# Other blocks transposed on TensorE, and another list of rank shifts for the planner, in a post-norm transformer block

## The chip, the core and the metric

The kernel runs on one core of a Trainium2 chip, as a single launch. The metric is the device time in microseconds of one execution. A core has five engines with queues of their own: TensorE (PE in the profile; PEld is its weight load), VectorE (DVE), ScalarE (ACT), GpSimd (POOL) and SyncE (SP), which here only issues transfers. All data is float32.

## The reference, cut to what matters

Two batches of 512 tokens of width 512 go through one layer:

```python
x = layernorm(x + attention(x))      # 32 query heads, 8 key/value heads, head size 128
x = layernorm(x + ffn(x))            # width 1376, silu(gate) * up, int32 weights with scales
# attention: q, k = rmsnorm(x Wq^T), rmsnorm(x Wk^T); v = x Wv^T
#            softmax(q k^T / sqrt(128) + slope_h * (j - i), masked to j <= i) v, then Wo
```

Every product over 512 or more is a matmul on TensorE. Transposes are needed twice in attention: the normed heads (so that the head size lies on partitions) and the probabilities (so that the keys lie on partitions).

## The kernel before

**Tiles.** A unit is one block of 128 tokens of one batch and one key/value head (group) `g` with its 4 query heads: `units` has 8 x 2 x 4 = 64 entries, and two neighbouring units make one of the 32 `pairs`. For each pair, `project` computes q, k and v of 256 tokens as seven products of half-size blocks (Strassen's scheme, `seven`, banks `pa`, `pb`, `pc`), with sums of blocks (`sums_x` of x, `sums_q` of the weights) made on DVE and POOL; pair 0 is projected by plain products (`project_plain`, bank `pp`, L856). `heads` squares, averages and norms the heads (`sq`, `ms`, `inv`), and turns them into `qT` and `kT`. `scores` computes a unit's scores (`sc`, L1252), the running maximum on DVE (L1261), the exponentials on ACT (L1277) and the division by the sum. `attend` turns the probabilities (`prT`) and multiplies by v (`pa`, L1397); the second unit of the last pair of a group also does the halves `px` and `pz` (L1429). `project_out`/`project_pair` multiply by Wo, `norm1` norms, and `ffn_up`/`ffn_down` follow. Batch 0 can start its feed-forward part while batch 1 is still in attention.

**Two ways of turning.** By default heads and probabilities are turned without TensorE: DVE transposes 32x32 squares (`squares`, L957, tile `st`; L1177 for heads), SP writes them to DRAM (`far`, L966; `far_q`, L1190) and reads them back in the order wanted (`prT`, L1374; `qT`, L1201). For the pairs in `NEAR = {0, 31}` TensorE transposes them instead (`ptq` and `ptk`, L1134 and L1149, 10 for a pair; `pt`, L1348), and DVE or ACT copies them out. Pairs in `NEAR` need their v in another row order (`vn`, loaded by SP).

**What sets the order.** Nothing is issued as it is written. `Work.add` collects about 8000 pieces of work, each with a rank (`prio`), its possible engines and a cost; `Work.order` places them one by one: among the ready ones, the one that can start first, then the one of lowest rank. So the engine for a piece, the order on each queue and the buffer are all a result of the ranks. Before that, `Work.shift` is called for each number in `SHIFTS`: the number seeds a random generator that draws a place in the ranks and moves the ranks of all work near it by random amounts. Loads have ranks too, so their order on the SP and ACT queues moves with them. The first loads are the four pieces of x (`load_x`, ACT queue, 128 rows each of `xT`, of which the first is split in two halves) and of the first group's weights (`load_qkv`, SP queue), rank -9 and up.

**Semaphores of transfers.** Each transfer signals one of eight semaphores in turn, over both queues; a transfer that is to use a semaphore again first waits, in its queue, for the one eight places before it to land.

Of the kernel before, what the change touches and what calls it, by code (L numbers as in the profile page):

```python
# [31 lines left out]
NQ = P // Q  # L32
# [6 lines left out]
LN_EPS = 1e-5  # L39
NEG_INF = -1e30  # L40
MAX_INIT = 3e38
NEAR = {0, 31}
PLAIN = 1
DEEP = HKV - 2
EARLY = 4
# [26 lines left out]
def pool_ts(n):  # L72
# [3 lines left out]
LAG = {"PE": 0.22, "DVE": 0.1, "ACT": 0.12, "POOL": 0.2, "SP": 0.1, "ACTQ": 0.1, "NONE": 0.0}  # L76
TABLE = 1.28
SHIFTS = (
    22000003, 22000016, 22000019, 22000030, 22000031, 22000059, 22000062, 22000085, 22000096,
    22000110, 22000180, 22000208, 22000219, 22000282, 22000333, 22000351, 22000369, 22000431,  # L80
    22000607, 22000642,
)
NORMED = {"DVE": dve(5 * HD) + 0.2, "POOL": pool_tt(5 * HD), "ACT": 5 * act(HD, True)}
WHO = ("DVE", "POOL", "ACT")
# [258 lines left out]
def post_ln_block(  # L343
# [110 lines left out]
    pairs = units[::2]  # L454
    NP = len(pairs)
    NU = len(units)
# [518 lines left out]
    def heads(p, prio):  # L975
# [67 lines left out]
        for r in range(2):  # L1043


            def normed(e, r=r):
                dst = sq[:, r]
                src = c(r)[:, : 5 * HD].rearrange("p (h d) -> p h d", h=G + 1)
                if p in NEAR:
                    dst = dst.rearrange("p h (r m) -> p h m r", m=NQ)  # L1050
                    src = src.rearrange("p h (m r) -> p h m r", m=NQ)
                if e == "ACT":
                    for h in range(G + 1):
                        nc.scalar.activation(  # L1054
                            dst[:, h], src[:, h], AF.Copy, scale=inv[:, r, h : h + 1]
                        )
                    return
                norms = inv[:, r].unsqueeze(2)
                if p in NEAR:
                    norms = norms.unsqueeze(3)  # L1060
                vec[e].tensor_tensor(dst, src, norms.to_broadcast(list(src.shape)), ALU.mult)

            W.add(
                {k: NORMED[k] for k in WHO},
                prio,
                normed,
                [(cb, (r, 0)), (cb, (r, 1)), (inv, r)],
                [(sq, r)],
                port=True,
            )  # L1070
# [2 lines left out]

        v2 = Buf(r_vs, f"vs_{p}")
        v2s[p] = v2
        users = [q for q in range(NP) if pairs[q][:2] == (g, b) and pairs[q][2] >= i]
        if any(q in NEAR for q in users):
            if (g, b) not in vns:
                vns[g, b] = Buf(r_v, f"vn_{g}_{b}")
            vn = vns[g, b]  # L1080
            for m in range(NQ):
                at = H2 * (m // 2) + m % 2
                load(
                    0.13 / NQ,
                    prio + 0.2,
                    lambda q, m=m, at=at, vn=vn: q.dma_start(
                        vn[ts(m, Q), i : i + 2, :], cb[at : at + H2 - 1 : 2, :, 1, 2 * HD :]
                    ),
                    [(vn, (i + r, m)) for r in range(2)],
                    [(cb, (r, 1)) for r in range(2)],  # L1090
                )
        if p in NEAR:
            for m in range(2):
                load(
                    0.02,
                    prio + 0.2,
                    lambda q, m=m: q.dma_start(
                        v2[H2 + m * Q : H2 + (m + 1) * Q, :], cb[m:H2:2, 0, 1, 2 * HD :]
                    ),
                    [(v2, m)],  # L1100
                    [(cb, (0, 1))],
                )
        else:
            copy_op(
                HD,
                prio + 0.2,
                lambda: v2[H2:, :],
                lambda: c(0)[:H2, 5 * HD :],
                [(cb, (0, 1))],
                [(v2, m) for m in range(2)],  # L1110
                ("ACT", "POOL"),
            )
        if any(q not in NEAR for q in users):
            if (g, b) not in vs:
                vs[g, b] = Buf(r_v, f"v_{g}_{b}")
            v = vs[g, b]
            for r in range(2):
                copy_op(
                    HD,
                    prio + 0.2,  # L1120
                    lambda r=r, v=v: v[:, i + r, :],
                    lambda r=r: c(r)[:, 5 * HD :],
                    [(cb, (r, 1))],
                    [(v, (i + r, m)) for m in range(NQ)],
                    ("ACT", "POOL"),
                )
        qT = qTs[p] = Buf(r_qT, f"qT_{p}")
        if p in NEAR:
            for r in range(2):
                pt = Buf(r_po, f"ptq_{p}_{r}")  # L1130

                def transposes(e, r=r, pt=pt):
                    for h in range(G):
                        nc.tensor.transpose(pt[:, ts(h, P)], sq[:, r, h, :], ident.tile)  # L1134

                W.add({"PE": G * TR}, prio + 0.4, transposes, [(sq, r), A(ident)], [A(pt)])
                copy_op(
                    S,
                    prio + 0.4,
                    lambda r=r: qT[:, r, :, : G * Q].rearrange("p a (h c) -> p a h c", h=G),  # L1140
                    lambda pt=pt: pt.tile.rearrange("p (h a c) -> p a h c", h=G, a=NQ),
                    [A(pt)],
                    [(qT, r)],
                )
            ptk = Buf(r_po, f"ptk_{p}")

            def transposes_k(e):
                for r in range(2):
                    nc.tensor.transpose(ptk[:, ts(r, P)], sq[:, r, G, :], ident.tile)  # L1149

            W.add({"PE": 2 * TR}, prio + 0.4, transposes_k, [(sq, 0), (sq, 1), A(ident)], [A(ptk)])

            def evict_k(e):
                dst = kT[:, i * P : (i + 2) * P].rearrange("p (m k r) -> p m k r", m=4, k=2)
                src = ptk[:, : 2 * P].rearrange("p (m r k) -> p m k r", m=4, k=2)
                if e == "ACT":
                    nc.scalar.activation(dst, src, AF.Copy, scale=kw[:, g, :])
                else:
                    nc.vector.tensor_scalar_mul(dst, src, kw[:, g, :])

            W.add(
                {"DVE": 0.48, "ACT": act(2 * P, True)},
                prio + 0.4,
                evict_k,
                [A(ptk), (kw, g)],
                [(kT, (i + r, x)) for r in range(2) for x in range(2)],
            )
            return
# [154 lines left out]
    def attend(u, prio):  # L1323
# [6 lines left out]
        key = f"{g}_{b}_{i}"  # L1330
        pr = pr_of[i]
        p, r = divmod(units.index(u), 2)
        values = lambda q: (vns if q in NEAR else vs)[g, b]
        v = values(p)
        for j in range(i + 1):
            prT = prTs[u, j] = Buf(r_prT, f"prT_{key}_{j}")
            a0 = 2 if j == i and r == 0 else 0
# [2 lines left out]
                reads += [(pr, ("x", a)) for a in range(2)]  # L1340

            n = (NQ - a0) * Q
            if p in NEAR:
                pt = Buf(r_po, f"pt_{key}_{j}")

                def transposes(e, j=j, pt=pt, a0=a0):
                    for a in range(a0, NQ):
                        nc.tensor.transpose(pt[:, ts(a - a0, P)], pr[:, a, ts(j, P)], ident.tile)  # L1348

                W.add({"PE": (NQ - a0) * TR}, prio, transposes, reads + [A(ident)], [A(pt)])  # L1350
                copy_op(
                    NQ * n,
                    prio,
                    lambda prT=prT, n=n: prT[:, : G * n].rearrange("p (h a q) -> p a h q", h=G, q=Q),
                    lambda pt=pt, n=n: pt[:, : G * n].rearrange("p (a h q) -> p a h q", h=G, q=Q),
                    [A(pt)],
                    [(prT, 0), (prT, 1)],
                )
                continue
# [65 lines left out]
        def halves(e):  # L1425
            for m, (q, j) in enumerate(both):
                prT = prTs[(g, b, j), j]
                for k, (bank, val) in enumerate(zip(banks, (values(q)[:, j, :], v2s[q].tile))):
                    nc.tensor.matmul(  # L1429
                        by_head(bank[:, ts(m, S // 2)]),  # L1430
                        lhsT=val[k * H2 : (k + 1) * H2],
                        rhs=by_head(prT[k * H2 : (k + 1) * H2, :])[:, :, :H2],
                        start=True,
                        stop=True,
                        tile_position=(k * H2, 0),
                        skip_group_check=True,
                    )

        reads = []
        for q, j in both:  # L1440
            reads += [(prTs[(g, b, j), j], m) for m in range(2)]
            reads += [(values(q), (j, m)) for m in range(NQ)] + [(v2s[q], m) for m in range(2)]
        W.add({"PE": 1.07}, prio + 0.4, halves, reads, [A(bank) for bank in banks])
        for m, (q, j) in enumerate(both):
            for k, bank in ((1, banks[0]), (0, banks[1])):
# [356 lines left out]
    for p in range(NP):  # L1802
# [3 lines left out]
        if p > 0 and fresh:  # L1806
            load_qkv(g, u - 14.0)
            load_o(g, u - 10.0)
        if p < PLAIN:
            project_plain(p, u - 2.4)  # L1810
        if fresh:
            sums_q(g, u - 3.0)
        if p > 0:
# [417 lines left out]
```

## Time and profile before

| | |
|---|---|
| median of 3 runs | 965.06 us (964.11 to 968.87) |
| profiled execution | 966.59 us, span 964.8 us |
| TensorE busy | 946.9 us, 98% of the span |
| VectorE, ScalarE, GpSimd busy | 75%, 50%, 54% |
| mean granted TensorE clock | 0.996 |
| transfers | 154.83 MB, 160 GB/s |

The page of the profile gives the busy time of each engine, then 40 slices of the span; a waits view lists, for each engine and line, what it sat idle for; a timeline lists instructions in order of time, neighbours of one kind merged, with the idle time before them in brackets. A float32 matmul instruction stands as two records. In a timeline the rows of a queue end in q (SPq, ACTq).

### The profile page before, as it was taken

How to read it: one execution, taken by the hardware profiler on the slowest of the kernel's cores; microseconds unless marked ns; L12 is line 12 of the kernel's file. 1: busy time of each engine (PE TensorE's matmuls, PEld its weight loads, DVE VectorE, ACT ScalarE, POOL GpSimd, SP SyncE). 2: the span in 40 equal slices, each digit the busy share in tenths (PEclk: the TensorE clock that was granted, in tenths of full speed). 3: DMA queues.
4: the chain of work that ended last, by engine and by line, in shares of the span. 5: the costliest groups of instructions: out<-in, count | busy, mean ns of one | idle time of the engine just before them, and what ended most of it. 6: DMA issues, size and time to landing. Idle time of an engine off the chain costs nothing.

```text
span 964.8 us, 14143 instructions
## 1 busy us (share of the span) xinstructions
PE 946.9 (98%) x4274; PEld 684.9 (71%) x4274; DVE 724.6 (75%) x1791; ACT 482.9 (50%) x1343; POOL 516.8 (54%) x587
## 2 busy tenths in 40 slices
PE   9899999999999999999999999999999999999997
PEld 5555666767666676667677767676777888878886
DVE  7777787878887888878877878777776766587554
ACT  3665655545764666555664655545653343434000
POOL 4752765475566658654674877765663522142120
PEclk9999999999999999999999999999999999999999
DMA  8258577555765586884747787567561323310001
GB/s 313 73 190 237 162 233 213 165 156 187 208 208 175 161 249 188 227 236 127 220 141 222 211 239 222 162 188 206 169 199 34 99 67 88 86 48 23 12 33 43
DMA packets 193099, 154.83 MB, mean 160 GB/s; under 512 B 27680, under 2 KB 176160, under 8 KB 191744
## 3 DMA queue, kind: packets, MB, share of 16 engines
q1 hardware_dynamic: 192160, 153.28, 53.3%
q8 instruction: 34, 0.56, 0.3%
q10 hardware_dynamic: 864, 0.66, 0.2%
q14 instruction: 41, 0.34, 0.1%
HBM read 96.28 MB, written 57.15 MB: 159 GB/s over the span
## 4 chain that ended last, share of the span: by engine, by line
PE 91%; DMA 4%; DVE 3%; issue 1%; SPq 0%; ACT 0%; ACTq 0%; POOLq 0%; DVEq 0%; POOL 0%
PE pa_q L736 16%; PE sc L1252 13%; PE pa L1397 11%; PE pa_h L736 8%; PE pb_q L736 8%; PE pa_o L1621 7%; PE pb_h L736 4%; PE pc_q L736 4%; PE pb_o L1621 4%; PE pa_d L736 4%; PE pa_o L736 2%; DMA prT<-far 2%; PE pc_h L736 2%; PE pc_o L1621 2%; PE pb_d L736 2%; PE px L1429 2%
## 5 line engine op out<-in xcount | busy, mean ns | idle before, releaser
L1277 ACT ACTIVATE pr<-pr,nmax 128x48 f32<-128x48 f32 (+15 forms) x256 | 133.2, 521 | 89.0 <-DVE nmax L1261 88.1
L1252 PE MATMUL sc<-kT,qT 128*128 128x176 f32 (+15 forms) x512 | 153.0, 408 | 0.9 <-ACT kT L1215 0.8
L1261 DVE CUSTOM_DVE_ANT_0 pr<-sc,bias 128x48 f32<-128x48 f32 (+15 forms) x256 | 110.0, 442 | 37.4 <-PE sc L1252 34.5
L1397 PE MATMUL pa<-prT,v 128*128 128x512 f32 (+1 forms) x300 | 126.3, 510 | 2.5 <-DMA prT<-far 2.5
L1252 PEld LDWEIGHTS sc<-kT,qT 128*128 128x128 f32 x512 | 87.3, 191 | 44.4 <-issue 18.5
L677 DVE TENSOR_TENSOR acc<-acc,pa_o 128x512 f32<-128x512 f32 (+2 forms) x128 | 72.5, 567 | 41.0 <-PE pa_o L1621 29.3
L1309 ACT ACTIVATE pr<-pr,rden 128x256 f32<-128x256 f32 (+11 forms) x200 | 85.7, 491 | 20.9 <-DVE rden L1292 20.6
L957 DVE STREAM_TRANSPOSE st<-pr 128x512 f32<-128x512 f32 (+1 forms) x150 | 90.4, 635 | 5.7 <-ACT pr L1309 2.5
L736 PE MATMUL pa_q<-tq,sx 128*128 128x384 f32 x248 | 91.1, 490 | 0.0
L837 ACT COPY c<-pa_q 128x384 f32<-128x384 f32 x85 | 40.4, 476 | 79.0 <-PE pa_q L736 72.4
L663 POOL TENSOR_TENSOR inv<-ms,nhalf 128x10 f32<-128x10 f32 (+1 forms) x33 | 64.5, 1956 | 16.2 <-DVE ms L1028 15.0
L1397 PEld LDWEIGHTS pa<-prT,v 128*128 128x128 f32 x300 | 53.3, 191 | 26.7 <-issue 5.6
L837 ACT COPY gu<-pa_h 128x256 f32<-128x256 f32 (+1 forms) x88 | 31.8, 369 | 74.3 <-PE pa_h L736 58.2
L1311 POOL TENSOR_SCALAR pr<-pr,rden 128x64 f32<-128x64 f32 (+10 forms) x88 | 41.5, 484 | 50.5 <-DVE rden L1292 50.2
L736 PEld LDWEIGHTS pa_q<-tq,sx 128*128 128x128 f32 x248 | 45.7, 191 | 30.4 <-issue 6.5
L1054 ACT ACTIVATE sq<-c,inv 128x128 f32<-128x128 f32 x170 | 53.4, 396 | 17.2 <-POOL inv L663 17.0
L991 ACT ACTIVATE sq<-c 128x640 f32<-128x640 f32 x64 | 45.4, 729 | 19.3 <-DVE c L1177 13.0
L1177 DVE STREAM_TRANSPOSE c<-sq 128x320 f32<-128x320 f32 x120 | 54.8, 487 | 0.1
L1014 DVE TENSOR_REDUCE ms<-sq 128x5 f32<-128x640 f32 x64 | 51.2, 811 | 4.5 <-ACT sq L991 4.4
L736 PE MATMUL pb_q<-w,xT 128*128 128x384 f32 x124 | 47.1, 503 | 3.4 <-DVE xT L677 3.4
L1621 PEld LDWEIGHTS pa_o<-ti,si 128*128 128x128 f32 x336 | 43.3, 192 | 8.5 <-issue 3.8
L1277 ACT ACTIVATION_READ_ACCUMULATOR pr<-pr,nmax 128x1 f32 x256 | 48.0, 187 | 0.0
(241 smaller groups left out, 2183.4 us busy)
## 6 DMA issues: line engine op xcount, KB each, us to landing
far<-st SPq DMA_DIRECT2D x120, 256.0 KB, 2.9
prT<-far SPq DMA_DIRECT2D x240, 128.0 KB, 3.5
far_q<-c SPq DMA_DIRECT2D x30, 640.0 KB, 3.8
qT<-far_q SPq DMA_DIRECT2D x60, 320.0 KB, 3.9
w<-in_wqkv_dram SPq DMA_DIRECT2D x39, 384.0 KB, 5.4
wo<-in_wot_dram SPq DMA_DIRECT2D x10, 1024.0 KB, 6.6
far<-st SPq DMA_DIRECT2D x30, 128.0 KB, 2.7
prT<-far SPq DMA_DIRECT2D x60, 64.0 KB, 2.9
```

The lines of the kernel that those rows point to most:

```text
L663: lambda e: nc.gpsimd.tensor_tensor(dst(), src(), nhalf[:, :n], ALU.pow),
L677: lambda e: vec[e].tensor_tensor(dst(), a(), b(), alu),
L736: nc.tensor.matmul(bank[:rows, :width], lhsT=a(fa, c), rhs=b(fb, c), start=(fresh and c == 0), stop=(c == depth - 1), skip_group_check=True,)
L837: nc.scalar.copy(dst(), src())
L957: {"DVE": dve(n)}, prio, lambda e: nc.vector.transpose(dst(), src()), reads, [A(st)]
L1177: lambda e, r=r, m=m: nc.vector.transpose(cb[:, m] .rearrange("p n w -> p (n w)")[:, :half] .rearrange("p (m r h d) -> p r h m d", m=2, r= ...
L1252: lambda e, a=a, w=w, sc=sc: nc.tensor.matmul(sc[:, :w], lhsT=qT[:, r, a, : G * Q], rhs=kT[:, :w], start=True, stop=True),
L1261: lambda e, a=a, w=w, sc=sc: nc.vector.tensor_tensor_reduce(out=pr[:, a, :w], in0=sc[:, :w], in1=bias[:, S - w :], scale=-(SHRINK**-g), sc ...
L1277: lambda e, a=a, w=w: nc.scalar.activation(pr[:, a, :w], pr[:, a, :w], AF.Exp, bias=nmax[:, a : a + 1], scale=-1.0, accum_out=den[:, a : a ...
L1309: nc.scalar.activation(dst, src, AF.Copy, scale=rden[:, a : a + 1])
L1397: lambda e, j=j, prT=prT, n=n: nc.tensor.matmul(by_head(po.tile)[:, :, P - n // G :], lhsT=v[:, j, :], rhs=late(prT, j, n), start=(j == 0) ...
L1621: nc.tensor.matmul(bank[:, ts(c, P)], lhsT=a(fa, c), rhs=b(fb, c), start=fresh and c == 0, stop=True, skip_group_check=True,)
```

## The change

The list `SHIFTS` of 20 numbers is replaced by one of 110 others. `NEAR` is split in two: the heads of pair 0 alone are transposed on TensorE (`NEAR_Q`), and the probabilities of units 0, 1 and 63 (`NEAR`, now counted in units). So the heads of pair 31 and the probabilities of unit 62 go by DVE and DRAM as all the others do. For unit 62, v is then also kept in the common row order. The rest follows from counting in units.

```diff
-NEAR = {0, 31}
+NEAR_Q = {0}
+NEAR = {0, 1, 63}
...
 SHIFTS = (
-    22000003, 22000016, 22000019, 22000030, 22000031, 22000059, 22000062, 22000085, 22000096,
...
+    42000001, 42000003, 42000019, 42000038, 42000046, 42000048, 42000080, 42000095, 42000168,
...
 )
@@ heads
             def normed(e, r=r):
-                if p in NEAR:
+                if p in NEAR_Q:
                     dst = dst.rearrange("p h (r m) -> p h m r", m=NQ)
...
-        users = [q for q in range(NP) if pairs[q][:2] == (g, b) and pairs[q][2] >= i]
-        if any(q in NEAR for q in users):
+        users = [w for w in range(NU) if units[w][:2] == (g, b) and units[w][2] >= i]
+        if any(w in NEAR for w in users):
...
-        if p in NEAR:
+        if 2 * p + 1 in NEAR:
             for m in range(2):
                 load(
...
-        if any(q not in NEAR for q in users):
+        if any(w not in NEAR for w in users):
...
-        if p in NEAR:
+        if p in NEAR_Q:
             for r in range(2):
                 pt = Buf(r_po, f"ptq_{p}_{r}")
@@ attend
-        values = lambda q: (vns if q in NEAR else vs)[g, b]
-        v = values(p)
+        values = lambda w: (vns if w in NEAR else vs)[g, b]
+        v = values(2 * p + r)
...
-            if p in NEAR:
+            if 2 * p + r in NEAR:
                 pt = Buf(r_po, f"pt_{key}_{j}")
@@ the loop over pairs
-        if p < PLAIN:
-            project_plain(p, u - 2.4)
+        if p == 0:
+
+            for q in range(PLAIN):
+                project_plain(q, 2 * q - 2.4)
```

With `PLAIN = 1` the last hunk issues the same work as before.

## The prediction

> **What bounds the kernel now.** First the page, for the bound:
>
> ```profile
> span 964.8 us, 14143 instructions
> PE 946.9 (98%) x4274; PEld 684.9 (71%) x4274; DVE 724.6 (75%) x1791; ACT 482.9 (50%) x1343; POOL 516.8 (54%) x587
> ...
> PE   9899999999999999999999999999999999999997
> ...
> PEclk9999999999999999999999999999999999999999
> ```
>
> TensorE has work in nearly every slice; the others do not. The order of work can therefore win only the 17.9 us in which TensorE stands still, what it loses at a lower clock, and the work taken off it. The waits of TensorE, over the span:
>
> ```profile
> PE pb_q L736 <- DVE xT L677: 3.4, 1, 3.4
> PE pa L1397 <- DMA prT<-far: 2.5, 4, 1.2
> PE pb_h L736 <- DVE gu L677: 1.5, 1, 1.5
> PE warm L543 <- POOL ident masks.py:199: 1.3, 1, 1.3
> PE sc L1252 <- ACT kT L1215: 0.8, 1, 0.8
> PE pz L1429 <- ACT aT L837: 0.6, 1, 0.6
> PE pp L856 <- DMA xT<-in_xt_dram: 0.5, 1, 0.5
> PE pa_o L736 <- DVE c L1177: 0.5, 1, 0.5
> PE pa L1397 <- ACT prT L837: 0.2, 1, 0.2
> ```
>
> They sum to 11.3 us; the rest is the end after the last matmul. One wait stands out. TensorE's timeline around it:
>
> ```profile
> 24.72 0.60 PE L1134 MATMUL ptq<-ident,sq 128*128 128x128 f32 x4
> 25.16 1.46 PE L736 MATMUL pa_q<-tq,xT 128*128 128x384 f32 x4
> ...
> 46.47 2.93 PE L736 MATMUL pb_q<-w,xT 128*128 128x384 f32 x4 [3.43 <-DVE xT L677]
> 49.20 2.77 PE L736 MATMUL pa_q<-w,xT 128*128 128x384 f32 x4
> 51.76 1.64 PE L736 MATMUL pa_q<-tq,sx 128*128 128x384 f32 x4
> 53.23 1.45 PE L736 MATMUL pc_q<-w,xT 128*128 128x384 f32 x4
> ```
>
> Four records of 128x384 normally follow one another in 1.29 us (53.23 to 54.52). After the wait of 3.43 us the same four take 2.73, 2.56 and 1.47 us: 2.89 us more. The granted clock there is 0.57 (47 to 53 us). So this one hole costs 6.3 us. Last, the transfers at the start, from the timeline, and their time to landing (for the loads of w):
>
> ```profile
> 0.72 3.75 SPq L475 DMA_DIRECT2D w<-in_wqkv_dram  x5
> 0.73 2.34 ACTq L501 DMA_DIRECT2D xT<-in_xt_dram  x5
> 4.36 2.75 PE L856 MATMUL pp<-w,xT 128*128 128x384 f32 x8
> ...
> 7.63 8.01 PE L856 MATMUL pp<-w,xT 128*128 128x384 f32 x24 [0.52 <-DMA xT<-in_xt_dram]
> ...
> DMA to landing us min/median/max: 2.7/5.4/6.0
> ```
>
> The first product starts at 4.36, halts 0.5 us for the second piece of x, and ends at 15.5.
>
> **The change part by part**, in the order that the built program has on each queue, priced by rows of the profiled execution (966.59 us). That execution stands 1.5 us above the median of 965.06; I take the sum from the median.
>
> *Transposes off TensorE.* Heads of pair 31: 8 + 2. Unit 62: 4 + 4 + 2. Four stand 0.44 us apart (24.72 to 25.16), so 20 x 0.11 = **-2.2 us**, all in a stretch (600 to 740 us) where TensorE hardly waits. In their place come 4 head transposes on DVE (0.49 each), 3 of probabilities (0.64), 12 transfers more on SP (680 for 668), two copies of v (0.30), and some 3.5 us of copies out of PSUM less. What hides it: between the last score of unit 62 and its first use of `prT` the changed order has 23.7 us of TensorE work (adding columns at 0.323 us for 384); the way itself is some 9 us (exponential 0.7, reciprocal 0.2, scale 0.5, transpose 0.6, `far` 2.9, `prT` 3.5). Heads of pair 31: 30.6 us of work between, for a way of the length that the other 30 pairs go with 20 to 52 us between; their one wait on it is the 0.8 for `kT`. Uncovered, it would cost the 7 us of the two transfers. I take 0.
>
> *The hole at 43 us.* It came from DVE's queue: the sum into `xT` for pair 3 stood behind a reduce of pair 2 that waited for ACT. In the changed order POOL makes this sum, behind the power for pair 1 (2.25), `ti` (1.01) and `wo` (1.27). From the last product of pair 1 the way is: add 0.55, copy of v 0.30, square 0.74, two reduces 1.64, then on POOL 0.27, `to` 0.99, two scales 0.66, 2.25, 1.01, 1.27, 0.73: 10.4, with six handovers of 0.1 about 11.0. TensorE has 11.6 us of work between. So **-6.3 us**, and for the thin margin **+0.3** (0 to 6.3: all of it back).
>
> *The start.* Here the new ranks look worse. x now comes in the order: second piece, back half of the first, fourth, front half of the first, third. w comes in the order: first piece in two halves, fourth, third, the two norm vectors, and only then the second. The plain product must go through its pieces in order. Its first matmul now needs what lies 192 KB deep in the queue of x: before, 128 KB of x was there by 4.4 us, 256 KB at 7.6; 192 KB lies between, say 5.9. The norm vector `kw` reuses the semaphore of that same half, so SP waits with it until 5.9, and the second piece of w, next on the queue, is issued at about 6.4. A load of w took 2.7 to 6.0 us; with most of the queue drained, 3.5. So it lands at 9.9; 24 records remain, 7.74 us: the end of the product moves from 15.5 to 17.7, **+2.2**. Lower bound: if bandwidth alone holds it (2.05 MB at the 250 to 390 GB/s of these slices), 9.0, +1.3. Upper: half at 7.5, w issued at 8.0, 5.9 to land: +6.1. Between 4.4 and 9.9 TensorE now stands still some 2.9 us in pieces; the hole at 43 lost 2.89 at the lower clock, so 0 to 2.9 here; I take **+0.8**, as the idle time is broken up. Start: +3.0 (1.3 to 9.0).
>
> On the clock, the Trainium skill speaks against this start too: "TensorE: Matmul & The Clock Gate", Part 1, says that the clock is halved after an idle window of about 3.4 us and restored after a busy one. The trace has the halving after a wait of 3.43 us, but begun before that wait was over. By the page alone no piece of the start is long enough: the 0.8 would be 0 and my sum 0.8 lower.
>
> *After the start.* DVE's sum into `xT` for pair 1 now stands behind a copy that waits for pair 1's first product (1.29) and a reduce (0.82): ready 3.2 us after the plain product, wanted after 2.6: **+0.7** with handovers (0 to 1.9). *Heads of pair 2.* The four loads of the next weights (1.57 MB) now go ahead of `far_q` on SP. Issue 2.1, `far_q` behind them at some 300 GB/s 7.3, `qT` 0.9 + 3.9, `kT` 0.8, and SP held some 3 us by `far` stores queued between the two `qT` reads: 18 to 19.4, for 18.4 us of TensorE work: **+1.0** (0 to 6, with a lower clock).
>
> *The other waits* (6.2 us without the hole, the start and `warm`). Nothing ties them to a place that the change keeps. The least work between a unit's last score and its first `prT` is 13.3 us in the new order (13.7 in the old, from unit 8 on), and the median 20.4 (20.7): no more slack than before. **-0.7** for the longer list (-6.2, all gone, to +6.2, doubled). The end is the same sequence: 0.
>
> Sum: -2.2 - 6.3 + 0.3 + 3.0 + 0.7 + 1.0 - 0.7 = -4.2, that is **960.9 us**.
>
> **Rivals.**
> 1. *The hole comes back (slower).* POOL is late with the sum for pair 3. For it: 10.4 us of chain with 11.6 of cover, and powers of 1.96 to 2.36 us. Against: TensorE itself arrives later after a slower start, and the chain's head moves with it. The price is the 6.3 less the 0.3 counted: 966.9. It decides from a wait of some 2.4 us, which with the lower clock after it costs the 4.5 us that were won.
> 2. *The start at its upper end.* Six more: 966.9 as well; with w landing at 13.9, or TensorE at half clock for a whole 3 us. For it: x and w both arrive out of order. Against: by then the queue of w holds one piece only.
> 3. *A clean run.* The start at its lower end and the other waits gone: -2.2 - 6.3 + 1.3 - 6.2 = 951.7. For it: TensorE waits for nothing from 300 to 640 us even now. Against: no more slack between the pieces.
> 4. *The way by DRAM is exposed* for unit 62 or pair 31, or another hole of the size of the old one opens elsewhere: +7, 968. Against: 23.7 and 30.6 us of cover.
>
> **How the numbers follow.** My forecast, a small gain (956 to 965): 0.55; rival 1: 0.15; rival 2: 0.10; rival 3: 0.12; rival 4: 0.08. The range 952 to 971 runs from rival 3 to rivals 1, 2 and 4 with 3 us to spare. A measurement of this kernel tells some 0.5% (4.8 us) from no change. Faster than that (under 960.2): 0.28 of the forecast's 0.55, and rival 3: 0.40. Slower (over 969.9): parts of rivals 1 (0.07), 2 (0.04), 4 (0.07): 0.18. The same: 0.42. The forecast's own range, 956 to 965, has both of the first two.
>
> **What would show it.** In the changed profile: the first plain product's 24 records should start near 10 us rather than 7.6, with a wait on a load of w (1.3 to 3 us in all before the product's end); the wait `pb_q` on `xT` near 43 us should be under 1 us and the clock there full; TensorE's busy time should fall by 2.2 plus some 2.9 us, and its records by 20, to 4254; the waits on `prT` should sum to 1 to 4 us. I am wrong if w's second piece lands by 8, if a wait over 2 us stands anywhere between 20 and 100 us, or if the sum of other waits leaves 0 to 12.

## The result, and the profile after

| | before | after |
|---|---|---|
| median | 966.19 us (964.11 to 968.87, 6 runs) | 953.47 us (952.38 to 955.17, 6 runs) |
| profiled execution | 966.59 us, span 964.8 us | 954.71 us, span 952.9 us |
| TensorE busy | 946.9 us | 940.2 us |

The ratio is 0.9867, 95% interval 0.9847 to 0.9888: 12.7 us faster, where 4.2 were forecast. The time lies inside the range, but the gain is three times the one that was worked out, so a step of the working failed. A part of the 12.7 us is the clock, which is not the same in every execution of one kernel: with a mean granted clock of 0.999 the changed kernel took 952.4 to 952.9 us (3 executions) and the kernel before 962.7 to 964.5 (5 of the 67 that stand beside the experiments), and at 0.995 or 0.996 the kernel before stands at 966.1 in the median.

The page of the changed kernel has for the span, the engines and the slices of TensorE:

```profile
span 952.9 us, 14098 instructions
PE 940.2 (99%) x4254; PEld 682.6 (72%) x4254; DVE 713.3 (75%) x1767; ACT 485.2 (51%) x1347; POOL 549.3 (58%) x608
...
PE   8999999999999999999999999999999999999997
```

The 20 records fewer are there. The first slice is worse than before (8), and the slice with the hole at 43 us is now full. TensorE's waits over the whole span (sum, times, longest):

```profile
PE pa L1408 <- DMA prT<-far: 2.7, 2, 2.1
PE pp L867 <- DMA w<-in_wqkv_dram: 1.8, 1, 1.8
PE warm L554 <- POOL ident masks.py:199: 1.3, 1, 1.3
PE pb_q L747 <- DVE ms L1039: 0.5, 1, 0.5
PE pp L867 <- DMA xT<-in_xt_dram: 0.4, 1, 0.4
```

Before, nine rows summed to 11.3 us; now five sum to 6.7. Besides the one of 3.4 us, the waits for `gu`, `kT`, `aT`, `c` and `prT<-ACT` are gone, which the prediction gave back only in part. One new wait has come, 2.1 us on `prT`. TensorE's timeline at the start, where the hole was, and at the new wait:

```profile
5.04 3.06 PE L867 MATMUL pp<-w,xT 128*128 128x384 f32 x8 [0.44 <-DMA xT<-in_xt_dram]
9.87 7.98 PE L867 MATMUL pp<-w,xT 128*128 128x384 f32 x24 [1.77 <-DMA w<-in_wqkv_dram]
17.68 1.45 PE L747 MATMUL pa_q<-w,xT 128*128 128x384 f32 x4
20.93 1.53 PE L747 MATMUL pb_q<-w,xT 128*128 128x384 f32 x4 [0.51 <-DVE ms L1039]
...
43.17 1.45 PE L747 MATMUL pb_q<-w,xT 128*128 128x384 f32 x4
...
688.09 2.05 PE L1408 MATMUL pa<-prT,v 128*128 128x512 f32 x2 [2.11 <-DMA prT<-far]
```

The 24 records start at 9.87, behind the load of w; the four records at 43.17 follow their neighbours at once and take the normal 1.45; at 688 two records take 2.05 where such a pair takes 1.02 elsewhere (49.21 us): the half clock after the wait.

**Where the 11.9 us between the two profiled executions went.** For each TensorE record I took the distance from its start to the next one's start, and what it exceeds the lower quartile for records of its bank and shape; summed by stretch this gives what waits and a slow clock cost there.

| stretch | before | after | difference |
|---|---|---|---|
| start of the first product | 4.36 | 5.04 | +0.7 |
| 0 to 20 us (with the wait of `pb_q`) | 0.8 | 3.0 | +2.2 |
| 40 to 60 us | 7.0 | 0.3 | -6.7 |
| 130 to 300 us | 6.7 | 2.0 | -4.7 |
| 300 to 640 us | 5.8 | 5.0 | -0.8 |
| 640 to 720 us | 5.1 | 5.9 | +0.8 |
| 860 to 900 us | 1.8 | 0.0 | -1.8 |
| the rest (20 to 40, 60 to 130, 720 to 860, from 900) | 1.7 | 1.7 | 0.0 |
| the records themselves | 925.1 | 923.7 | -1.4 |
| behind the last matmul | 6.1 | 5.9 | -0.3 |

The sum is -11.9 (the rounded rows add to -12.0). How it is split depends a little on the quartile, each kernel's own or one for both: by it 130 to 300 us gains 4.6 to 5.0, 300 to 640 us 0.6 to 1.3, and the records 0.5 to 2.2. The start, the hole and the transposes came out close to the working. What it did not have is -4.7 and -1.8, at places that neither the transposes nor the start touch.

### The profile page after: what moved, and what is told of

Its sections match the earlier page's. It is cut to its first block, busy times and chain, and to the rows that moved or that the text cites. A ratio compares the mean times of both kernels' runs of the same rounds, so it can differ in the third digit from the quotient of the medians.

```text
span 952.9 us, 14098 instructions
## 1 busy us (share of the span) xinstructions
PE 940.2 (99%) x4254; PEld 682.6 (72%) x4254; DVE 713.3 (75%) x1767; ACT 485.2 (51%) x1347; POOL 549.3 (58%) x608
## 4 chain that ended last, share of the span: by engine, by line
PE 96%; DMA 2%; SPq 1%; DVE 0%; issue 0%; POOLq 0%; DVEq 0%
PE pa_q L747 17%; PE sc L1263 13%; PE pa L1408 12%; PE pb_q L747 8%; PE pa_h L747 8%; PE pa_o L1632 8%; PE pb_h L747 4%; PE pc_q L747 4%; PE pb_o L1632 4%; PE pa_d L747 4%; PE pa_o L747 3%; PE pc_o L1632 2%; PE pc_h L747 2%; PE pb_d L747 2%; PE px L1440 2%; DMA prT<-far 2%
## 5 line engine op out<-in xcount | busy, mean ns | idle before, releaser
L1263 PE MATMUL sc<-kT,qT 128*128 128x512 f32 (+15 forms) x512 | 154.1, 409 | 0.0
L1408 PE MATMUL pa<-prT,v 128*128 128x512 f32 (+1 forms) x306 | 129.6, 512 | 2.7 <-DMA prT<-far 2.7
L1320 ACT ACTIVATE pr<-pr,rden 128x64 f32<-128x64 f32 (+12 forms) x221 | 95.4, 495 | 23.1 <-DVE rden L1303 22.8
L848 ACT COPY c<-pa_q 128x384 f32<-128x384 f32 x73 | 34.5, 473 | 54.2 <-PE pa_q L747 47.4
L688 POOL TENSOR_TENSOR so<-aT,aT 128x512 f32<-128x512 f32 x23 | 29.3, 1274 | 32.8 <-PE pa_o L1632 31.7
L1322 POOL TENSOR_SCALAR pr<-pr,rden 128x64 f32<-128x64 f32 (+7 forms) x67 | 31.1, 473 | 29.4 <-DVE rden L1303 28.3
```

The lines of the kernel that those rows point to most:

```text
L688: lambda e: vec[e].tensor_tensor(dst(), a(), b(), alu),
L848: nc.scalar.copy(dst(), src())
L1263: lambda e, a=a, w=w, sc=sc: nc.tensor.matmul(sc[:, :w], lhsT=qT[:, r, a, : G * Q], rhs=kT[:, :w], start=True, stop=True),
L1320: nc.scalar.activation(dst, src, AF.Copy, scale=rden[:, a : a + 1])
L1408: lambda e, j=j, prT=prT, n=n: nc.tensor.matmul(by_head(po.tile)[:, :, P - n // G :], lhsT=v[:, j, :], rhs=late(prT, j, n), start=(j == 0) ...
```

## The experiments

Two questions. Is the start a plain loss (theory A), or does a later TensorE wait less later on, so that the loss pays itself back (theory B)? And what took out the waits from 130 us on: the longer list of shifts (theory L) or the new structure with fewer transposes at the end (theory S)? In several kernels a function `moved` takes the finished order and moves single pieces of work in it; everything else stays as it was planned. Each run stands beside runs of the kernel before on the same chip; the ratios are to those.

### The start by itself

The changed kernel with the first twelve transfers in the order of the kernel before, and the kernel before with those of the changed one:

```diff
+    # in the changed kernel; the other one has the other order
+    first = [wrote("xT_0", (0, 0)), wrote("w_0", (0, 0)), wrote("xT_0", (0, 1)), wrote("w_0", (1, 0))]
+    first += [wrote("xT_0", (1, 0)), wrote("w_0", (0, 1)), wrote("xT_0", (2, 0)), wrote("xT_0", (3, 0))]
+    first += [wrote("w_0", (0, 2)), wrote("w_0", (0, 3)), wrote("qw", 0), wrote("kw", 0)]
+    at = sorted(placed.index(o) for o in first)
+    for k, o in zip(at, first):
+        placed[k] = o
```

> The changed kernel with its plan as it is, but the twelve first transfers issued in the order of the kernel before (first piece of x and w first, the norm vectors last). Theory A (the late start of the plain product is a plain loss, and the waits after 60 us went because the new ranks place the work better): the wait on w at 9.9 us goes, the product ends near 15.5 instead of 17.7, and the whole falls by 2.2 to 2.9 us, from 953.5 to about 951. Theory B (TensorE starting later is what lets the transfers and the other engines get ahead, so that the later waits are absorbed): the time stays within 0.7 us of 953.5, and the 2 us come back as waits behind the start.

> The kernel before with its plan as it is, but the twelve first transfers issued in the order of the changed kernel. Theory A: it loses what the start loses, 2 to 4 us, to about 969, with the hole at 43 us and the waits of 130 to 300 and 640 to 720 us as they were. Theory B: the hole at 43 us and the later waits shrink, and the time stays at 966 or falls below it.

Measured: the changed kernel with the old start 951.72 us (0.9859, 0.9837 to 0.988), 1.8 less than the changed one. The kernel before with the new start 969.37 us (1.0037, 1.0023 to 1.005), 4.2 more than the 965.14 beside it. Theory B falls: in the second kernel the hole at 43 us stands as it was, 3.4 us, only 5 us later, and most of the waits behind it too. The 1.8 us are hardly the earlier product's, though; and as the intervals of the two ratios overlap, they are themselves not shown. The timeline of TensorE in the changed kernel with the old start:

```profile
4.79 2.99 PE L867 MATMUL pp<-w,xT 128*128 128x384 f32 x8 [0.19 <-DMA xT<-in_xt_dram]
8.07 8.01 PE L867 MATMUL pp<-w,xT 128*128 128x384 f32 x24 [0.29 <-DMA xT<-in_xt_dram]
15.91 1.45 PE L747 MATMUL pa_q<-w,xT 128*128 128x384 f32 x4
...
20.65 1.53 PE L747 MATMUL pb_q<-w,xT 128*128 128x384 f32 x4 [2.00 <-DVE ms L1039]
```

The product ends 1.8 us earlier (`pa_q` at 15.91 for 17.68), and `pb_q`, which the same two products precede, starts only 0.3 earlier (20.65 for 20.93). The wait is now 2.0 us, for DVE's sum into `xT`. DVE's timeline in the same kernel:

```profile
10.94 1.50 DVE L568 SCALAR_TENSOR_TENSOR kw<-kw,qw 128x1 f32<-128x1 f32 x1 [1.05 <-DMA kw<-in_knw_dram]
...
20.09 0.41 DVE L688 TENSOR_TENSOR xT<-xT 128x256 f32<-128x256 f32 x1
```

The old order of transfers has the norm vector `kw` last. DVE waits 1.05 us for it, and from there to the sum the chain that ended last runs through DVE alone. In the changed kernel `kw` is there when DVE wants it (9.82 us), and the pieces of this queue start 0.9 us earlier, until a copy has to wait for TensorE. So the edit does two things: it brings w earlier and the norm vector later. 1.5 of the 1.8 us were lost again by the second, and 0.3 is left of the start in this pair of executions. An order that has both early was not run. Their spans still differ by 3.1 (949.8 for 952.9), because the wait at 688 us was also shorter in that one (1.4 us for 2.1; the stretch from 640 to 720 us cost 3.2 for 5.9). A second estimate of the start's worth comes below, from two kernels that have no such wait: 0.8.

In the other kernel the same order of transfers costs far more at the start, since TensorE waits in one piece:

```profile
7.42 13.51 PE L856 MATMUL pp<-w,xT 128*128 128x384 f32 x32 [2.82 <-DMA qw<-in_qnw_dram]
20.76 1.45 PE L736 MATMUL pa_q<-w,xT 128*128 128x384 f32 x4
```

32 records at 0.323 are 10.3 us; here they take 13.3 to the start of `pa_q`. The bound for the half clock at the start (0 to 2.9) was right in kind: it is about 0.2 in the changed kernel's profile (its first record takes 0.54 us) and about 3 here.

### The hole by itself

The kernel before, with DVE's sums for pair 3 ahead of its transposes of heads:

```diff
+    at = min(placed.index(wrote("c_1", ("turned", r, m))) for r in range(2) for m in range(2))
+    sums = [o for o in placed[at:] if o["writes"] and o["writes"][0] in (("xT_1", (0, 3)), ("sx_1", (1, 1)))]
+    for o in sums[:2]:
+        placed.remove(o)
+    placed[at:at] = sums[:2]
```

> The kernel before with its plan as it is, but DVE makes the sum into xT for pair 3 and the sum that follows from it before the head transposes of pair 1, instead of after the two reduces of pair 2. My term in the prediction (the hole of 3.43 us and the half clock after it are worth 6.3 us by themselves): 960. Rival (the hole hid other work: the scores of unit 2 need kT, which was there at about 52 us): TensorE waits 2 to 4 us at the first scores of unit 2 instead, and the gain is 0 to 4 us: 962 to 966.

Measured 964.79 us (0.9993, 0.9978 to 1.0008): nothing won. The timeline shows why:

```profile
43.39 1.45 PE L736 MATMUL pb_q<-w,xT 128*128 128x384 f32 x4
...
52.10 2.93 PE L736 MATMUL pa_q<-tq,sx 128*128 128x384 f32 x4 [3.38 <-ACT c L837]
```

The wait before `pb_q` is gone, and 3.38 us stand four products later, with the same half clock after it (2.93 us for four records). ACT's copy out of PSUM stands there behind its scaling of pair 2's heads, which waits for POOL's power. So a second kernel also puts that scaling, and the first transpose that needs it, behind the copies:

```diff
+    copy = next(o for o in placed if o["eng"] == "ACT" and ("c_3", (0, 1)) in o["writes"])
+    late = [[o for o in placed if o["eng"] == "ACT" and ("sq_2", 0) in o["writes"]][-1], wrote("c_2", ("turned", 0, 0))]
+    late = [o for o in late if placed.index(o) < placed.index(copy)]
+    for o in late:
+        placed.remove(o)
+    at = placed.index(copy) + 1
+    placed[at:at] = late
```

> The kernel before with the sums for pair 3 moved ahead of the transposes of heads, as before, and now ScalarE's two copies out of PSUM also ahead of the scaling of pair 2's heads, which is where the hole came up again. If these two queues were all that was late: no hole from 40 to 60 us, 957 to 960. If the keys of unit 2, which come through DRAM, are late as well: a third wait, for kT at the scores near 55 us, of 2 to 3.4 us, and 961 to 965.

Measured 964.59 us (0.9991, 0.9973 to 1.0008). The wait has moved a second time:

```profile
49.34 1.56 PE L736 MATMUL pa_q<-tq,sx 128*128 128x384 f32 x4 [0.78 <-ACT c L837]
53.19 1.32 PE L1252 MATMUL sc<-kT,qT 128*128 128x304 f32 x4 [2.30 <-POOL kT L1217]
```

So three things were late at the same place: the sum (due at 43), the copy (at 48) and the keys that come through DRAM (at 51). The prediction named the first. Its price of 6.3 us was right for the changed kernel, where all three are in time, but moving the one named work would not have earned it. What cured the hole is the rank of all the work around it.

### Ranks alone, structure alone

The changed kernel with the 20 shifts of the kernel before, and the kernel before with the 110 of the changed one:

```diff
 SHIFTS = (
-    42000001, 42000003, 42000019, 42000038, 42000046, 42000048, 42000080, 42000095, 42000168,
+    22000003, 22000016, 22000019, 22000030, 22000031, 22000059, 22000062, 22000085, 22000096,
...
```

> The changed kernel with the list of 20 shifts of the kernel before: the move off TensorE alone. Theory L (the ranks took the waits, the move off TensorE only its own 2.2 us): ratio 0.995 to 1.003, about 963 to 967, with TensorE waits after the start of 6 to 14 us and some holes where the kernel before has them. Theory S (the structure: with fewer transposes at the end and one earlier, the work around them has more slack, whatever the ranks): under 958, with waits after the start under 5 us.

> The kernel before with the list of 110 shifts of the changed one: the ranks alone. Theory L, if the ranks carry over to a program that differs in three units: the start's loss of about 3, no hole at 43 us and no waits from 130 to 300 us, so some 2 to 4 us above the changed kernel, 955 to 958. If ranks fit only the very program that they were tried on: 962 to 972, with new waits of over 1 us in places where neither kernel has one. Theory S: no better than the kernel before, 963 or more, because the structure is the old one.

Measured: structure alone 968.99 us (1.0038, 1.0025 to 1.0052); ranks alone 961.37 us (0.9955, 0.9943 to 0.9968). The kernel before beside them took 965.50. Theory S falls: with the old list the move off TensorE loses 3.5 us. TensorE's waits in that kernel:

```profile
PE pa L1398 <- DMA prT<-far: 4.7, 5, 1.8
PE pb_q L737 <- DVE xT L678: 3.4, 1, 3.4
PE pb_h L737 <- DVE gu L678: 1.6, 1, 1.6
...
PE sc L1253 <- ACT kT L1216: 1.0, 1, 1.0
PE pa_o L737 <- DMA wo<-in_wot_dram: 0.7, 1, 0.7
```

The hole and nearly all the other waits of before are there, and those on `prT` have grown from 2.5 us (1.5 to 2.0 in the three variants of the kernel before) to 4.7: in the stretch from 640 to 720 us they are 3.3 for 1.5. These are not the waits of the unit that now goes through DRAM. In the program's order the two largest, 1.84 us at 699.9 and 0.88 at 711.6, belong to units 58 and 59, which went through DRAM before too; unit 62's products start at 745.69 us and wait for nothing. The transposes were won and more was lost elsewhere; by which piece of work is not followed further.

In the kernel with the ranks alone:

```profile
PE pa_h L746 <- ACT gu L847: 3.6, 5, 1.5
...
PE pp L866 <- DMA xT<-in_xt_dram: 0.8, 2, 0.5
PE pp L866 <- DMA w<-in_wqkv_dram: 0.8, 1, 0.8
PE pa_o L746 <- DVE acc L687: 0.5, 1, 0.5
PE pb_q L746 <- DVE ms L1038: 0.5, 1, 0.5
```

Up to 300 us, where the two programs do the same work, it has the start of the changed kernel, no hole at 43 and no wait from 130 to 300 us (the excess there is 1.9; before 6.7, after 2.0). From 720 to 860 us, behind the place where its structure differs, it waits 4.4 us that neither kernel has: five waits for ScalarE's `gu` and two for `acc`. By the same measure the stretch costs 6.7, and about 0.4 in both kernels.

So L is right where the programs are the same. Behind that point the two kernels do not have the same ranks, though they have the same list: `shift` draws a number for each new place and cost in the order in which the pieces were added, so a piece that only one program has changes the draws that follow. Worked out from the code of the two kernels, which have some 4850 pieces each, the pieces common to both have the same ranks up to unit 62's scores, and all 810 behind these have others; with the old list it is the same. So the 4.4 us do not say that the new ranks fit only their own program, and the two runs split ranks from structure only ahead of that point. Swapped in this way, either part alone moves the time by +3.5 and -4.1, -0.6 if they added; together they give -12.7.

### The list cut short

The changed kernel with 55, 20 and none of its 110 shifts:

```diff
-    42000530, 42000532, 42000548, ... 42026349,      (the last 55; the last 90; all)
```

> The changed kernel without any shift. Theory L: the worst of the four, 966 or more, waits after the start of 12 us or more. Theory S: within 5 us of the changed kernel, under 959.

> The changed kernel with only the first 20 of its 110 shifts. Theory L: the waits fall as the list grows, so between the kernel without shifts and the changed one, 957 to 966, waits after the start of 5 to 12 us. Theory S: within 3 us of the changed kernel, 951 to 957.

> The changed kernel with the first 55 of its 110 shifts. Without any it takes 980.8, with 20 963.3, with 110 953.5. If every part of the list takes out waits: 955 to 960, TensorE waits after the start of 3 to 7 us. If the list beyond the first 20 does nothing that the chip shows but for one lucky place: 960 to 966.

Measured: none 980.80 us (1.0169, 1.0132 to 1.0206), 20 963.25 us (0.9985, 0.9973 to 0.9998), 55 962.92 us (0.9971, 0.9957 to 0.9984), all 110 953.47 us. The first 20 bring 17.6, the next 35 nothing that can be told, the last 55 9.5. So the waits do not fall evenly with the length of the list, as the first case of the expectation for 55 had it; the time lies in its second. The waits of the kernel with 20, and then of the one with 55, show what still stands:

```profile
PE pp L857 <- DMA w<-in_wqkv_dram: 3.9, 1, 3.9
PE pb_o L737 <- POOL aT L678: 1.9, 1, 1.9
PE sc L1253 <- DVE nmax L1262: 1.6, 1, 1.6
```

```profile
PE pp L861 <- DMA w<-in_wqkv_dram: 4.2, 1, 4.2
PE pa L1402 <- DMA prT<-far: 3.1, 3, 2.1
PE sc L1257 <- DVE nmax L1266: 1.6, 1, 1.6
```

In both the first product waits 4 us in one piece for the first load of w, and starts at 8.4 and 8.8 us. That start alone is 3.4 to 3.8 us later than in the changed kernel. The later shifts repaired it, to the start that the prediction called worse. Without any shift the waits on `prT` sum to 10.9 us.

### The new wait at 688 us

In the changed kernel's timeline of SP:

```profile
677.58 0.35 SPq L541 DMA_DIRECT2D wo<-in_wot_dram  x1
678.01 3.53 SPq L1385 DMA_DIRECT2D prT<-far  x4
```

A load of 1 MB for later (`wo`) is issued just ahead of four reads into `prT`; it took 8.1 us to land, and the read that TensorE waits for 7.0. One kernel issues this load behind the reads; another has that and the old start as well.

```diff
+    load = [o for o in placed if o["eng"] == "SP" and ("wo_6", 0) in o["writes"]][1]
+    placed.remove(load)
+    placed.insert(placed.index(wrote("prT_6_1_2_1", 1)) + 1, load)
```

> The changed kernel with its plan as it is, but the load of wo (1 MB) at 677.6 us is issued behind the four reads into prT that follow it on SP. If the wait of 2.1 us at 688 us comes from these reads lying behind the megabyte in the transfer engines (7.0 us from issue to landing), the wait and the half clock after it go: 3.6 us less, 950. If it comes from the store of unit (6,1,2) being late, the wait stays and the time is 953.5.

> The changed kernel with the first transfers in the order of the kernel before and the load of wo that stood ahead of the reads into prT at 678 us behind them. If the two places have nothing to do with each other, both gains: 1.8 for the start and 1.3 to 3.6 for the hole at 688 us, 948 to 950.5. If what is won early is lost again at the next late piece: 951 to 952.5, no better than either edit alone.

Measured: 952.24 us (0.9860, 0.9837 to 0.9882) and 951.44 us (0.9852, 0.9828 to 0.9876). With the load moved the waits on `prT` are

```profile
PE pa L1408 <- DMA prT<-far: 1.5, 3, 0.8
```

and 0.7 of them from 640 to 720 us, for 2.7; that stretch cost 2.3 for 5.9. So the load was the cause: the 128 KB reads around it took 7.0 us to land in the median, and 3.8 with the load behind them. What it costs differs between executions. With the load in front the wait here was 2.1 us in the changed kernel, 1.4 with the old start and 0.7 in the kernel with more transposes below, and only behind the first was the clock halved. Of the 3.6 us the median shows 1.2; in the same execution a wait of 0.8 at 553 us appeared that the changed kernel's profile lacks. With both edits:

```profile
PE pb_q L747 <- DVE ms L1039: 2.0, 1, 2.0
PE warm L554 <- POOL ident masks.py:199: 1.3, 1, 1.3
PE pa L1408 <- DMA prT<-far: 0.9, 2, 0.7
```

The hole at 688 is gone and the wait that replaced the start's is there: 951.4, the expectation's second case. Between the two, which differ in the order of the first transfers alone, lie 0.8 us, an estimate, as they ran on two chips and the intervals of their ratios overlap. It is the lowest median of all, 2.0 under the changed kernel, but the interval of its ratio overlaps that of the changed kernel's, so it is not shown to be faster.

### The price of a transpose

The changed kernel with each of the 16 transposes of unit 63 issued four times:

```diff
                     for a in range(a0, NQ):
-                        nc.tensor.transpose(pt[:, ts(a - a0, P)], pr[:, a, ts(j, P)], ident.tile)
+                        for _ in range(4 if p == 31 else 1):
+                            nc.tensor.transpose(pt[:, ts(a - a0, P)], pr[:, a, ts(j, P)], ident.tile)
```

> The changed kernel with each of the 16 transposes of probabilities of unit 63 issued four times into the same place: 48 more on TensorE. At the 0.11 us a piece of the prediction: +5.2, 957 to 960. If transposes there are hidden beside waits for others: +0 to 2.

Measured 957.79 us (0.9916, 0.9897 to 0.9935): +4.3 for 48, 0.09 each. TensorE's busy time says 0.11 each:

```profile
PE 945.5 (99%) x4302; PEld 688.3 (72%) x4302; DVE 713.2 (75%) x1767; ACT 484.8 (51%) x1347; POOL 549.4 (57%) x608
```

945.5 for 940.2, 5.3 us for 48 more. On a TensorE that hardly waits a transpose costs its spacing; 20 of them are 1.8 to 2.2 us.

## Why the prediction was right or wrong

- **The other waits (-0.7): the step that failed.** Measured -6.4 (-5.6 to -7.4 by the quartile): the stretches from 20 us on without the hole. That is about the lower bound of this term, -6.2. In the view of waits, 6.1 us before (the prediction has 6.2) became 2.7, of which 2.1 are new; the rest is in gaps too short for the view and in the clock. It was argued with "Nothing ties them to a place that the change keeps", and, since the least and the median work between a unit's last score and its first `prT` had hardly changed, with "no more slack than before". Both sentences are about averages. The waits were nine single events, each with a queue and a cause of its own. One is easily followed: at 134 us TensorE waited 0.55 for ScalarE's copy of `aT`, which stood behind two squares that in turn waited for DVE's transposes. In the changed kernel that copy is done as soon as its product is (121.61 us) and four records of scores stand between it and the first `px`. At 865 us POOL's sums of 1.5 and 1.7 us ran beside DVE's `sg` and `hT`, which took 1.95 and 2.02 us instead of 0.74 each, and `pb_h` waited 1.5 for them; near that place in the changed order POOL does nothing from 850.2 to 857.2 us, and the `sg` and `hT` that DVE makes in this time take 0.74 each. The order of the changed program was known, and the hole at 43 was followed through it instruction by instruction; these were not. The run with the ranks alone shows for 130 to 300 us, where programs and ranks are both the same, that it was the ranks that removed the waits (1.9 us for 6.7); for the wait at 865 us, where the ranks are not the same, it does not. None of the prediction's signs of being wrong came: the 0 to 12 us that it allowed these waits had room for this outcome too.
- **The heads of pair 2 (+1.0):** 0. `qT` and `kT` were in time; the excess from 40 to 60 us is 0.3. The working had 18 to 19.4 for 18.4, the lower end was right.
- **The hole (-6.3, residue +0.3):** -6.7, no residue. POOL's sum was in time with the 0.6 us of margin. Right for this program; but the cause that was named was one of three, as the two moves in the kernel before show.
- **The start (+2.2 and +0.8):** the landing of w's second piece at 9.9 us and the product's end at 17.7 are exactly as worked out (9.87 and 17.68). The half clock, 0.8, was 0.2. By "TensorE: Matmul & The Clock Gate", Part 1, of the Trainium skill, as the prediction reads it, it would have been 0, which is nearer. But that is luck in part: in two other kernels with the same start the records ran at half pace until 7.0 and 7.4 us, and TensorE then waited less for w, so that the product ended no more than 0.2 us later. As a plain loss the term was too simple: the order that brings w earlier brings the norm vector later, and most of the time won is lost again at `pb_q`.
- **The wait of `pb_q` (+0.7):** 0.67 by the excess, 0.5 by the view of waits. Right.
- **The transposes (-2.2):** 1.8 to 2.2 by their own measurement. The way by DRAM at 0 was right: unit 62's products start at 734.95 us in the changed kernel and wait for nothing. What the working did not have is a wait of another unit: the one of 2.1 us at 688 us is unit 58's, whose way did not change. A `prT` read was counted at its usual length (3.5 us), and this one took 7.0 behind a load of 1 MB on the same queue.
- **The rivals.** 1 and 4 did not come; a wait of the size of rival 4's kind came at 688 us, 2.1 us and not 7. Rival 2 did not come in the changed kernel, though its mechanism did in the kernels that wait for the start in one piece. Rival 3, "a clean run" (951.7), had the answer but for the start.

What stays open: why the list of 110 fits so well. That it was selected on the very program is a likely reason, but how the shifts were chosen was not seen, and no run gives the same ranks to another program at its end.

## What to carry to other kernels

When a change alters a planner's ranks, follow every wait of the profile through the new order, each with its queue, as one does with the largest; a term "other waits, unchanged on average" is not an estimate. A hole in a full engine is often several late things at one place, and curing the first only shows the second, so its price is earned only when the whole neighbourhood moves. A list of random shifts and the program that draws from it are one thing: here either swapped alone gave +3.5 and -4.1 us, and both together -12.7, and where the programs differ the same list is another set of ranks.

## What the runs showed of the hardware

The length of a wait alone did not decide the clock. Two waits of 2.0 (the changed kernel with the old start) and 2.3 us (the kernel before with sums and copies moved) left the granted clock full; a wait of 2.1 us at 688 us in the changed kernel halved it for 3.4 us.

The traces' own record of the clock shows what did. In all fourteen it changes, from its first entry (at 4.25 to 13.72 us) on, only at whole multiples of 3.41 us. The windows view, cut along these multiples, has the busy time of TensorE first behind the length, and the granted clock in the column before the last two. First the changed kernel at 688 us, then the kernel before at its hole:

```profile
684.59:688.00 3.41, 1.39 (x8) 1.06 (x6) 2.36 (x10) 1.12 (x6) 0.77 (x2) 1.00 1.20 213
688.00:691.41 3.41, 3.33 (x7) 2.15 (x8) 0.28 (x2) 1.22 (x5) 0.37 (x1) 0.50 0.68 225
```

```profile
41.87:45.29 3.42, 1.18 (x4) 0.38 (x2) 2.59 (x7) 2.09 (x5) 3.28 (x4) 1.00 0.27 106
45.29:48.70 3.41, 2.23 (x4) 1.32 (x5) 1.95 (x5) 0.43 (x2) 2.26 (x2) 0.50 0.48 146
48.70:52.11 3.41, 3.41 (x7) 1.88 (x6) 2.76 (x7) 1.25 (x5) 2.13 (x4) 0.50 0.42 132
```

And the windows with the waits of 2.0 and 2.3 us, behind which the clock stayed full:

```profile
18.79:22.20 3.41, 1.55 (x5) 0.94 (x6) 2.53 (x7) 0.98 (x4) 3.33 (x6) 1.00 1.03 411
```

```profile
49.22:52.64 3.42, 1.56 (x4) 0.68 (x4) 2.95 (x7) 1.63 (x6) 1.68 (x3) 1.00 0.66 192
```

Over all fourteen traces, up to the last 10 us, every window of a full clock with TensorE busy for 1.42 us or less was followed by a halved one, and of those with 1.49 us or more one alone. So a wait costs the half clock or not by where the edges fall in it, and they lie differently in each execution: the first entry is at 4.33 us in the kernel before and at 6.95 in its variant with the sums moved, whose start is the same. At 43 us the halved window itself was busy for only 2.23 us, and a second one followed; behind a halved window of 3.01 us or more the clock was full again. The one exception is in the structure alone, 2.24 us busy from 131.93 to 135.34 us and a clock of 0.50 in the next window; its cause is open.

"TensorE: Matmul & The Clock Gate", Part 1, of the Trainium skill has the clock halved by a whole idle window of some 3.4 us that does not start with the wait. The multiples of 3.41 us agree; but a window with 1.4 us of work in it is not idle, so on this point the measurement stands against it.

At the start the windows view can mislead: before the first entry of the record it shows 1.00. In the kernel before with the new transfers the records of the first product follow one another at 0.64 us up to 13.31 us and at 0.32 from 13.66 on, and the first entry is at 13.37; 3.0 us were lost, and the view has 1.00 in every window from 7.4 to 18 us. A half pace at the start is therefore read from the distances of the records rather than from the clock's column.
